# A two-layer selective scan over eight images: the short scan's gate in place, its running sums from PSUM, its result stored once per half, and the next image's map loaded inside the scan

## The chip, the cores and the metric

The kernel runs on one core of one Trainium2 chip. The metric is the device time of one launch in microseconds (us). Three runs of the kernel before took 12600.73, 12612.84 and 12614.98 us; their median is 12612.84 us. One further execution was recorded by the hardware profiler; it took 12615.41 us, and its span, from the first instruction to the last, is 12613.3 us.

The engines go by these names in the profile: PE is TensorE (matmul), PEld its weight loads, DVE is VectorE, ACT is ScalarE, POOL is GpSimd, and SP is SyncE, which here issues nearly all DMAs. Each engine works through its own instructions in order. SBUF is the on-chip memory, PSUM the memory that matmuls write.

## What is computed

Eight images of 64 x 64 positions and 96 channels pass two layers. Each layer normalizes, projects to 2 x 192 channels, convolves (3 x 3, each channel alone), and scans the 4096 positions in four directions (rows, columns, and both backwards) with 16 states for each of the 192 channels. Then come a layer norm, a gate by `silu(z)`, a projection back to 96 channels, and the sum with the input. The two layers differ in the scan. The first is an exact recurrence; the second divides running sums by a decay, which is cut off by a small constant:

```python
# layer 0, per step
dA = jnp.exp(d_t[..., None] * A)
h = dA * h + d_t[..., None] * B_e * u_t[..., None]
y_t = jnp.sum(h * C_e, axis=-1)

# layer 1, one direction; s1 = rows, s3 = columns
def _ssm_scan(u, ...):
    dt = jax.nn.softplus(dt @ dt_proj_w + dt_proj_b)
    A = -jnp.exp(A_log)
    log_dA = jnp.einsum('bld,dn->bldn', dt, A)
    dB_u = jnp.einsum('bld,bln->bldn', dt, B_mat) * u[..., None]
    decay = jnp.exp(jnp.cumsum(log_dA, axis=1))
    h = decay * jnp.cumsum(dB_u / (decay + 1e-12), axis=1)
    y = jnp.einsum('bldn,bln->bld', h, C_mat)
    return y + u * D_skip
...
y = y1 + y2 + back(y3) + back(y4)
y = _layernorm(y, ln_g, ln_b).reshape(B, H, W, D_INNER)
return (y * jax.nn.silu(z)) @ out_proj_w
```

In layer 1 the term `decay / (decay + 1e-12)` dies away along the sequence, so the kernel scans only the first 160 positions of each direction (fewer for the faster states), and multiplies them by a gate, `0.5 * (1 + tanh(0.5 * (A * cumsum(dt) + log 1e12)))`. This is the **short scan**. At the end the kernel looks at the smallest decay that it met and, should the cut not have been allowed, computes the second layer again in a general way; with these inputs that part doesn't run.

## The kernel before

**Tiling.** The 192 channels are two halves `h` of 96, and each half three groups `g` of 32. A group's 32 channels times 4 states fill 128 partitions, and a **set** is one group with 4 of the 16 states over 1024 positions. One image's long scan (layer 0) has 4 directions x 4 stretches x 2 halves x 3 groups x 4 sets = 384 sets. From the second image on (`b >= 1`), 6 **short sets** follow (2 halves x 3 groups), which are the layer-1 scan of the image before; a short set holds all 16 states in 960 positions. Images are numbered 0 to 7 here.

**The order.** `scan_rows` (from L408) writes the order of the work out by hand. Step `n` issues, for each engine, the stages of neighbouring sets: loads for set n+5 (`fetch`, L509), the decay of set n+1 (`fill`, L843: ScalarE, into one of two PSUM tiles), `drive` of set n+1 (ScalarE copies the input term into a single PSUM tile), `release` of set n-4 (ScalarE copies the finished sums out of the accumulator `acc`, of which there is one), `gate` of set n+1, the multiply and scan of set n (`advance_set`: VectorE, L892, L895, L898, L903), the product with C of set n-1 (`read_out`: GpSimd, L920, into one of four tiles `out`), and the sum over states of set n-3 (`collect`: TensorE, L933 and L956, into `acc`). Then come the stages that `plan` holds for that step: they prepare later work on the same engines.

**Jobs.** A half of a stretch is a job of 12 sets. While the sets of job m run, the job m+2 is prepared, by `ready` for long and `short_ready` (L719) for short jobs. The steps of `short_ready` count from the job's start; the two short jobs are prepared from steps 359 and 371. Its matmuls all use one PSUM bank (`pmisc`, tag `mm`). At steps 6 and 7 TensorE forms dt in that bank (`total`, L760), at steps 7 and 8 ScalarE copies it to `ln` (`delta`, L769), at step 9 GpSimd multiplies it by the input (`product`, L772) and VectorE forms both running sums from `ln` (`running`, L781, 320 elements each, one of them backwards), at step 10 ScalarE copies the sums' heads and scales their ends (`lowest`, L505 and L794), and at step 11 they are stored to DRAM. From there `fetch` loads them back, replicated over the states, as `dt_rep`, `dtu_rep` and `cum_rep`; the first two have two buffers each.

**The gate.** `gate` (L858) takes one of the four `out` tiles, writes the gate into it (L869), and L895 multiplies the set by it. `read_out` then uses the same tile for its product.

**The short result.** `release` copies `acc` to a tile `y_short` (L974, one buffer) and stores its four quarters to `ys_far` in DRAM by four DMAs of SP (L978). In the phase between the images `short_sum` loads `ys_far` back in one DMA (L1750), and `patch` (L1712, from step 7 of that phase) adds it.

**The convolution beside.** `conv_beside` computes the convolutions of layer 0 for the next image and of layer 1 for the image before, in pieces, during the scan, in the same `pmisc` bank: nine taps in three steps (L1023), ScalarE's curve (L1033), VectorE's product out of the bank (L1036), and a store to `xc_far` in DRAM. `windows` says at which steps; the two last pieces of images 1 to 6 start 9 steps into the jobs that begin at steps 359 and 371.

**Between the images.** `between` loads the next image's map from `xc_far` in four quarters (L1767), at steps 0, 9, 11 and 13, and runs `out_phase`: 16 chunks of 512 positions (8 of layer 0 of this image, 8 of layer 1 of the one before) through stages with fixed lags: sum (GpSimd, L1580), mean (TensorE, L1516), centring (VectorE, L1593), square, variance and so on. Beside them `first_deltas` prepares the next scan; its first stages are the projection of the next map (L560) at steps 2 and 3. After the last image `finish` takes the place of `between`; it has no next map.

## Time and profile before

| what | value |
|---|---|
| median of three runs | 12612.84 us |
| profiled execution | 12615.41 us |
| VectorE's running sums of the short jobs (L781) | 28, 789 to 7414 ns |
| short gates (L869) | 168 instructions, 423 to 923 ns |
| ScalarE idle before L869 until an `out` tile | 45.4 us in 14 waits |
| ScalarE idle before L974 until a store of `y_short` | 70.4 us in 21 waits |
| TensorE idle before L560 until the map | 64.7 us in 6 waits |
| TensorE's granted clock, mean | 0.80 |

A group row of the profile reads: line, engine, operation, output `<-` inputs with their shapes, count, then the busy time and the mean of one in ns, then the idle time before and what ended it. A row in order of time reads: start, duration, engine, line, operation, output `<-` inputs, count of merged instructions, and in brackets the idle time before with what ended it. "SPq" is the queue of SyncE, whose rows are issues of DMAs. In the table by stretch a row has the stretch, its length, the busy time of each engine, then TensorE's granted clock, the mean busy share of the 16 DMA engines and their GB/s. The releaser is inferred, and may be wrong where an instruction waits for several things.

One image takes about 1540 us, of which the scan with its short sets is about 1390 and the phase between about 150.

### The profile page before, as it was taken

To read this page: it belongs to the slowest core of one execution; us is meant where nothing else is said; L and a number is where in the kernel's file an instruction comes from. 1 tells how busy PE (TensorE), PEld (TensorE's weight loads), DVE (VectorE), ACT (ScalarE), POOL (GpSimd) and SP (SyncE) were. 2 spreads that over 40 slices of the span, in tenths; PEclk is the share of its full clock that TensorE was granted. 3 is DMA by queue.
4 is the path that set the end of the run, shared out by engine and by line. 5 is a ranking of instruction groups with operands and counts; after the bars stand their busy time and mean duration, and the time that the engine had idled before them with its cause. 6 is when DMAs were issued, how large, how long until landed. Compare 5 with 4: busy or idle time off the path is not lost. (4 is left out here: it accounts for less than half of the span.)

```text
span 12613.3 us, 134470 instructions
## 1 busy us (share of the span) xinstructions
PE 9519.2 (75%) x44284; PEld 3021.0 (24%) x44284; DVE 11031.8 (87%) x6870; ACT 9693.0 (77%) x15131; POOL 10513.1 (83%) x4802
## 2 busy tenths in 40 slices
PE   5875588876887778887788777887688886786566
PEld 1221122222222222222222222222222222222122
DVE  6999899996999969999699987999779997899966
ACT  4888778786888868878688877888778886788864
POOL 3999899995999859998699977999779996799964
PEclk8877788787888778877888878888788787887676
DMA  3444444444444444444444444444444444444430
GB/s 95 164 158 154 137 150 160 157 158 131 164 158 162 141 131 163 162 157 149 138 165 153 159 147 136 164 158 160 148 141 164 148 153 143 144 162 157 155 112 23
DMA packets 667346, 1853.80 MB, mean 147 GB/s; under 512 B 186840, under 2 KB 199262, under 8 KB 666541
## 3 DMA queue, kind: packets, MB, share of 16 engines
q1 hardware_dynamic: 659469, 1832.53, 44.1%
q10 hardware_dynamic: 7168, 12.59, 0.3%
q8 instruction: 351, 5.75, 0.2%
q14 instruction: 358, 2.93, 0.1%
HBM read 1533.82 MB, written 311.02 MB: 146 GB/s over the span
## 5 line engine op out<-in xcount | busy, mean ns | idle before, releaser
L920 POOL TENSOR_TENSOR out<-set,c_rep 128x1024 f32<-128x1024 f32 x3114 | 7290.0, 2360 | 954.3 <-PE acc L956 305.2
L903 DVE TENSOR_TENSOR_SCAN set<-decay,state,set 128x1024 f32<-128x1024 f32 x2304 | 5365.5, 2345 | 416.3 <-ACT decay L856 198.8
L856 ACT ACTIVATE decay<-dt_rep,w_a 128x1024 f32<-128x1024 f32 x3072 | 3419.3, 1114 | 298.5 <-DVE set L903 292.6
L892 DVE TENSOR_TENSOR set<-drive,b_rep 128x1024 f32<-128x1024 f32 x2346 | 2812.5, 1199 | 44.1 <-DMA b_rep<-x_dblr 33.6
L1023 PE MATMUL ps_conv<-edged,taps 96*96 96x512 f32 (+1 forms) x4032 | 2418.1, 739 | 30.3 <-ACT z L615 27.8
L956 PE MATMUL acc<-out,w_gather 128*32 128x256 f32 x24576 | 2285.0, 482 | 21.4 <-POOL out L920 21.3
L903 DVE TENSOR_TENSOR_SCAN set<-decay,set 128x1024 f32<-128x1024 f32 x768 | 1744.9, 2286 | 222.1 <-ACT decay L856 143.7
L882 POOL TENSOR_TENSOR set<-dtu_rep,b_rep 128x1024 f32<-128x1024 f32 x768 | 1809.5, 2356 | 99.0 <-DMA b_rep<-x_dblr 47.5
L947 PE MATMUL acc<-map,w_eye 96*32 96x256 f32 x4608 | 570.3, 577 | 1591.9 <-ACT map L986 1359.1
L986 ACT COPY map<-acc 32x256 f32<-32x256 f32 x3072 | 1470.9, 479 | 46.6 <-PE acc L956 6.0
L956 PEld LDWEIGHTS acc<-out,w_gather 128*32 128x32 f32 x24576 | 784.6, 131 | 1954.4 <-issue 1256.1
L1023 PEld LDWEIGHTS ps_conv<-edged,taps 96*96 96x96 f32 (+1 forms) x4032 | 713.3, 196 | 1345.3 <-issue 1211.7
L914 ACT COPY state<-set 128x1 f32<-128x1 f32 x2304 | 426.3, 185 | 758.2 <-DVE set L903 751.3
L634 PE MATMUL ps_sp<-z,w_eye 96*96 96x512 f32 x960 | 644.0, 758 | 305.6 <-ACT ln L643 256.0
L655 POOL TENSOR_TENSOR dtu<-ln,map 96x1024 f32<-96x1024 f32 x256 | 670.6, 2620 | 236.5 <-DVE ln L651 133.1
L875 ACT COPY drive<-dtu_rep 128x1024 f32<-128x1024 f32 (+1 forms) x810 | 808.0, 998 | 35.0 <-DMA dtu_rep<-dtu_far 32.1
L602 PE MATMUL ps_dt<-x_dbl,w_dtw 7*96 7x512 f32 x1024 | 589.9, 657 | 311.9 <-ACT z L615 151.0
L947 PEld LDWEIGHTS acc<-map,w_eye 96*32 96x32 f32 x4608 | 102.1, 122 | 2059.0 <-ACT map L986 1757.0
L634 PE MATMUL ps_sp<-dtu,w_eye 96*96 96x512 f32 x960 | 552.5, 660 | 0.0
L634 PE MATMUL ps_sp<-ln,w_eye 96*96 96x512 f32 x960 | 537.8, 644 | 0.0
L614 ACT ACTIVATE dt<-ps_dt 96x512 f32<-96x512 f32 x512 | 303.0, 592 | 276.8 <-PE ps_dt L602 257.3
L634 PE MATMUL ps_sp<-dt,w_eye 96*96 96x512 f32 x960 | 508.9, 613 | 0.0
(236 smaller groups left out, 9622.7 us busy)
## 6 DMA issues: line engine op xcount, KB each, us to landing
dt_rep<-dt_far SPq DMA_DIRECT2D x768, 512.0 KB
dtu_rep<-dtu_far SPq DMA_DIRECT2D x768, 512.0 KB
b_rep<-x_dblr SPq DMA_DIRECT2D x256, 512.0 KB
c_rep<-x_dblr SPq DMA_DIRECT2D x256, 512.0 KB
b_rep<-x_dblc SPq DMA_DIRECT2D x256, 512.0 KB
c_rep<-x_dblc SPq DMA_DIRECT2D x256, 512.0 KB
dt_far<-ln SPq DMA_DIRECT2D x256, 384.0 KB
dtu_far<-dtu SPq DMA_DIRECT2D x256, 384.0 KB
```

Source lines behind the costliest of these rows:

```text
L634: nc.tensor.matmul(job["ps"][:C, :], w["eye"], job[term][:, halves[s]], start=i == 0, stop=i == 3,)
L655: nc.gpsimd.tensor_tensor(like(job["dtu"], col), like(job["dt"], col), positions(xc[:, h, :], col, t0, T), ALU.mult,)
L856: nc.scalar.activation(s["decay"], s["group"]["dt"], AF.Exp, scale=rate)
L875: nc.scalar.copy(s["group"]["drive"], s["group"]["dtu"])
L882: nc.gpsimd.tensor_tensor(s["buf"], s["group"]["dtu"], b, ALU.mult)
L892: nc.vector.tensor_tensor(s["buf"], s["group"]["drive"], b, ALU.mult)
L903: nc.vector.tensor_tensor_scan(ordered(s["buf"], unit), ordered(s["decay"], unit), ordered(s["buf"], unit), 0.0 if unit["nth"] == 0 else s ...
L920: nc.gpsimd.tensor_tensor(s["out"], s["buf"], s["unit"]["c", s["i"]], ALU.mult)
L947: nc.tensor.matmul(acc, lhs[:, GC * g : GC * (g + 1)], positions(old[:, h, :], unit["column"], unit["t0"] + at, n), start=True, stop=False ...
L956: nc.tensor.matmul(acc, w["gather"], s["out"][:, at : at + n], start=False, stop=s["i"] == NS - 1, skip_group_check=True,)
L986: nc.scalar.copy(yk, like(acc, unit["column"]))
L1023: nc.tensor.matmul(job["ps"][:C, :], taps[l][:k, h, tap, :], edged[:k, tap // 3 : tap // 3 + rows, tap % 3 : tap % 3 + WW], start=tap == 0 ...
```

## The change

Five things change, all at the end of an image's scan or at the start of the phase that follows.

1. `gate` writes in place over the replicated running sums (`cum_rep`); L895 reads them from there. `read_out` takes an `out` tile for short sets as it does for long ones.
2. `running` reads dt from the PSUM bank and not from `ln`. The backward half is summed at step 8, straight from the bank that `total(1)` left; for the forward half a new matmul with the identity (`again`, step 8) brings `ln` into the bank again, and its sum follows at step 9. As the bank is in use longer, the last two convolution pieces of images 1 to 6 start one step later (`at + 10`).
3. `release` gathers the three groups of a half in one tile, which shares its buffer with `conv_out`, and stores it by one DMA when the third is there. `ys_far` changes its layout, and `short_sum` loads it by six DMAs, at steps 2 and 3.
4. The next map's four quarters are loaded by SP at steps 376, 378, 380 and 388 of the scan (`next_map`), and no more in `between`.
5. The four stages of the first projection in `between` come one step earlier.

```diff
@@ scan_rows
-                    release(at(-4), y, work)
-                    gate(at(1), work)
+                    release(at(-4), y, beside)
+                    gate(at(1))
@@ short_ready
+        def again(s):
+            job["v"] = bank(s, "ps_again")
+            lhs, src = w["eye"], job["ln"][:, halves[s]]
+            nc.tensor.matmul(job["v"], lhs, src, start=True, stop=True)
+
         def running(s):
-            if s == 0:
+            if s == 1:
                 job["cum"] = tile_of("dt0")
-            at = slice(0, 2 * HEAD)
+            src, out = job["v"][:, : 2 * HEAD], job["cum"][:, halves[s]][:, : 2 * HEAD]
             if s == 1:
-                at = slice(BLOCK + 2 * HEAD - 1, BLOCK - 1, -1)
-            nc.vector.tensor_tensor_scan(
-                job["cum"][:, at], ones_reset, job["ln"][:, at], 0.0, ALU.mult, ALU.add
-            )
+                src, out = src[:, ::-1], out[:, ::-1]
+            nc.vector.tensor_tensor_scan(out, ones_reset, src, 0.0, ALU.mult, ALU.add)
...
             (8, lambda: delta(1)),
+            (8, lambda: running(1)),
+            (8, lambda: again(0)),
             (9, product),
             (9, lambda: running(0)),
-            (9, lambda: running(1)),
@@ gate, advance_set, read_out
-            s["out"] = work.tile([P, T], F32, name="out", bufs=4)[:, :HT]
...
-                nc.scalar.activation(out, src, AF.Tanh, bias=half_log, scale=rate)
+                nc.scalar.activation(cum, cum, AF.Tanh, bias=half_log, scale=rate)
...
-            nc.vector.scalar_tensor_tensor(buf, s["out"], 1.0, buf, ALU.add, ALU.mult)
+            nc.vector.scalar_tensor_tensor(
+                buf, s["group"]["cum"], 1.0, buf, ALU.add, ALU.mult
+            )
...
-            if not s["unit"]["short"]:
-                s["out"] = work.tile([P, T], F32, name="out", bufs=4)
+            s["out"] = work.tile([P, T], F32, name="out", bufs=4)[:, : s["unit"]["n"]]
@@ release
-            part = work.tile([P, HEAD], F32, name="y_short", bufs=1)
+            if g == 0:
+                unit["y"] = beside.tile([P, MM], F32, tag="conv_out", name="y_short")
+            part = unit["y"][:, g * HEAD : (g + 1) * HEAD]
             nc.scalar.mul(part, s["group"]["acc"][:, :HEAD], 0.5)
-            dst = ys_far[unit["b"]][GC * g : GC * (g + 1), h, :]
-            for k in range(K):
-                at = slice(k * HEAD, (k + 1) * HEAD)
-                nc.sync.dma_start(dst[:, at], part[GC * k : GC * (k + 1), :])
+            if g == NG - 1:
+                nc.sync.dma_start(ys_far[unit["b"]][h], unit["y"][:, : NG * HEAD])
@@ windows
-                found.append((at + 9, (3, 3, 3), 1))
+                found.append((at + 10, (3, 3, 3), 1))
@@ beside
+    def next_map(b, i):
+        if i == 0:
+            maps[b] = keep.tile([C, NH, L], F32, name="map")
+        at = slice(i * T, (i + 1) * T)
+        nc.sync.dma_start(maps[b][:, :, at], xc_far[b][:, :, at])
...
+                for i, step in enumerate((376, 378, 380, 388)):
+                    plan.setdefault(step, []).append(lambda i=i: next_map(b + 1, i))
@@ short_sum
-        put(1, nc.sync.dma_start, ys, ys_far[b])
+        def load_sums(h, g):
+            dst = ys[GC * g : GC * (g + 1), h, :].rearrange("c (k a) -> c k a", a=HEAD)
+            src = ys_far[b][h, :, g * HEAD : (g + 1) * HEAD]
+            src = src.rearrange("(k c) a -> c k a", c=GC)
+            nc.sync.dma_start(dst, src)
+
+        for h in range(NH):
+            for g in range(NG):
+                put(2 + h, load_sums, h, g)
@@ between
-        xc = keep.tile([C, NH, L], F32, name="map")
+        xc = maps[b + 1]
...
-            put(0, load, 0)
...
-            for i in range(1, NT):
-                put(7 + 2 * i, load, i)
...
-                steps = (2, 3, 3, 4) + (4, 5, 5, 6, 6, 7, 7, 6, 8, 9, 9)
+                steps = (1, 2, 2, 3) + (4, 5, 5, 6, 6, 7, 7, 6, 8, 9, 9)
```

## The prediction

> **What bounds the kernel now.** I read the page's first part, then the groups of instructions, then the order of time on each engine at one place where the changed code runs (the end of the second image's scan, 2820 to 2980 us), then the same place in the other images, and last the busy time by stretch for the DMA share. The page's chain of waits puts 0% on everything and says nothing.
>
> ```profile
> span 12613.3 us, 134470 instructions
> PE 9519.2 (75%) x44284; PEld 3021.0 (24%) x44284; DVE 11031.8 (87%) x6870; ACT 9693.0 (77%) x15131; POOL 10513.1 (83%) x4802
> L781 DVE TENSOR_TENSOR_SCAN dt<-ones_reset,ln 96x320 f32<-96x320 f32 x28 | 106.3, 3835 | 0.8 <-PE ps_sp L760 0.8
> ```
>
> VectorE is the bound: in the long scan it goes without a pause from multiply (1.20 us) to scan (2.35 us). The changed code runs only in the last 31 of an image's 390 sets and at the entry of the phase between two images. So the average is of no use; VectorE (DVE) there:
>
> ```profile
> 2875.98 1.20 DVE L892 TENSOR_TENSOR set<-drive,b_rep 128x1024 f32<-128x1024 f32 x1
> 2877.28 2.35 DVE L903 TENSOR_TENSOR_SCAN set<-decay,state,set 128x1024 f32<-128x1024 f32 x1
> 2879.54 7.30 DVE L781 TENSOR_TENSOR_SCAN dt<-ones_reset,ln 96x320 f32<-96x320 f32 x2
> ...
> 2926.82 1.16 DVE L895 SCALAR_TENSOR_TENSOR set<-out,set 128x960 f32<-128x960 f32 x1 [3.99 <-ACT out L869]
> 2928.01 2.20 DVE L898 TENSOR_TENSOR_SCAN set<-decay,set 128x480 f32<-128x480 f32 x2
> ...
> 2935.15 1.16 DVE L895 SCALAR_TENSOR_TENSOR set<-out,set 128x960 f32<-128x960 f32 x1 [3.89 <-ACT out L869]
> ```
>
> Two running sums hold VectorE 7.30 us. The gates of short sets 5 and 6 are 4 us late. ScalarE (ACT) and TensorE (PE) say why:
>
> ```profile
> 2919.15 2.36 ACT L986 COPY map<-acc 32x256 f32<-32x256 f32 x4
> 2924.77 2.02 ACT L869 ACTIVATE out<-cum_rep,half_log,a_half 128x640 f32<-128x640 f32 x4 [3.26 <-POOL out L920]
> 2933.10 2.02 ACT L869 ACTIVATE out<-cum_rep,half_log,a_half 128x640 f32<-128x640 f32 x4 [3.26 <-POOL out L920]
> 2941.78 0.30 ACT L974 ACTIVATE y_short<-acc 128x160 f32<-128x160 f32 x1 [2.91 <-DMA ys_far<-y_short]
> 2946.31 0.30 ACT L974 ACTIVATE y_short<-acc 128x160 f32<-128x160 f32 x1 [4.23 <-DMA ys_far<-y_short]
> ```
>
> ```profile
> 2921.61 3.07 PE L933 MATMUL acc<-out,w_gather 128*32 128x160 f32 x32 [15.58 <-ACT map L986]
> 2946.76 1.73 PE L933 MATMUL acc<-out,w_gather 128*32 128x160 f32 x32 [2.80 <-ACT y_short L974]
> 2948.42 1.96 PE L1516 MATMUL ps_mean<-y_sum,w_avg 96*96 96x512 f32 x4
> 2960.88 3.67 PE L560 MATMUL ps_proj<-map,w_wx 96*78 96x512 f32 x4 [10.51 <-DMA map<-xc_far]
> 2964.35 1.72 PE L1516 MATMUL ps_mean<-y_sum,w_avg 96*96 96x512 f32 x2
> ```
>
> Gate 5 starts 0.09 us after the 3.07 us collect of set 1 has ended (2921.61 + 3.07 = 2924.68): it waits for that collect to free one of the four `out` tiles, not for GpSimd (POOL), which the row names. Gate 6 waits likewise for set 2. After the gates a chain of collect, `y_short` copy and its store runs to 2948.5; TensorE, in order, then meets the projection, which waits 10.5 us for the map. SyncE (SP) issues that load late, behind 24 small stores:
>
> ```profile
> 2929.86 21.70 SPq L978 DMA_DIRECT2D ys_far<-y_short  x24
> 2954.34 0.59 SPq L1767 DMA_DIRECT2D map<-xc_far  x1
> ```
>
> The same pattern stands in images 2 to 7 (the last has no next map). In image 0, without a short scan, the map is in time.
>
> **What the skill says.** The Trainium skill, SBUF — State Buffer, Who interferes with whom: a VectorE instruction with two SBUF inputs contends with a GpSimd instruction that reads SBUF, one with a single SBUF input does not. The trace agrees: L781, both inputs in SBUF, takes 789 to 7414 ns, L892, one input in PSUM, an even 1.20 us. PSUM — Partial Sum Buffer, PSUM bank collisions raise a hardware error: accesses to a bank are to be ordered by semaphore; in the changed program as built the sum read from PSUM waits for ScalarE, so for the copy (L769) of the same bank; nothing before shows this wait. DMA: Bandwidth & Descriptors, Anatomy of one DMA (told of transfers issued from GpSimd): about 2 us are fixed, mostly the receipt; here, issued from SyncE, a copy that needs a 4 x 20 KB store complete waits 2.9 us. TensorE: Matmul & The Clock Gate, Part 1: an idle array runs at half clock; the same 32 matmuls take 3.07 us after a pause and 1.73 us in a run.
>
> **The change, part by part** (times in the frame of image 1).
>
> Running sums. Each pair costs VectorE 7.2 to 8.1 us now (2879.54 to 2886.77; the other 13 alike). From PSUM a sum should take its shortest time now, 0.79 us, 1.6 us a pair; L892 and L898 (1.14 us for 480, PSUM decay) show that one PSUM operand keeps GpSimd out. But the first sum now comes one step earlier and waits for the second L769 copy, behind four L986 copies. VectorE reaches that spot at 2824.79 and 2875.98; L769 ends at 2827.47 and 2877.94: waits of 2.7 and 2.0 us (3.4 for one of image 2, 4.1 in image 5, 5.0 in image 7). Behind the wait on VectorE stands the next set's multiply, and behind that GpSimd and ScalarE. So a pair saves 7.3 - 1.6 - 2.7 = 3.0 us, a little more or less by image: 6.2 an image. Bounds for the wait: 0 and 5. The added matmul (L760 rows, 0.7 to 1.0 us) waits for VectorE, but TensorE has idle time of 5 to 10 us there. What is late next is nothing: the decays are there.
>
> Convolution one step later. Its bank is needed for the copy of `ln`, so it starts at step 10. Its third part now comes behind a collect that waits for L986, and its product (L1036) one set later. The next job's first matmul needs that bank; ScalarE stands before L740 (3.17 us now) and the next decay is queued behind it. Step by step: L1036 ends 2853.0 instead of 2849.5, matmul 2.0, two reads 1.2, decay 1.1: 2857.4, where the scan now starts at 2854.33. Loss 2.7 to 3.1, I take 2.7, since a decay wait of 0.36 lies in it; bounds 0 and 4. Images 1 to 6 only.
>
> Gate in place. No new tile is taken, so gates 5 and 6 need no collect. Gate 5 follows L986 at 2921.5 (before: 2924.8), then decay 6 and drive 2.9, copy 0.3, gate 6 ends 2928.7 (before 2935.1); its last product leaves GpSimd at 2934.4 (before 2940.9). Gate and multiply cost what they did: the tile stays in SBUF.
>
> One store a half. The copies of sets 2, 3, 5 and 6 no longer wait for a store; that of set 4 waits for one of 240 KB, and its collect hides that. Collect chain: set 2 2926.9 to 2930.0, then set by set 2.25 to 3.5 us (1.73 or 3.07 + 0.3 + gaps of 0.2), set 6 ends about 2940.8 instead of 2948.5: 7.7 us an image. 24 issues of SP become 2; six loads instead of one in the next phase are 3 us of SP, with no one waiting (used at step 7).
>
> Map beside the scan. Four loads of 768 KB; by program order the first three are issued near 2860, where
>
> ```profile
> core 0: us, PE busy (x) PEld busy (x) DVE busy (x) ACT busy (x) POOL busy (x), PEclk, DMA share, GB/s
> 2860.00:2870.00 10.00, 6.20 (x37) 2.31 (x38) 6.07 (x4) 9.70 (x11) 6.56 (x3) 0.66 0.33 100
> 2910.00:2915.00 5.00, 0.00 (x0) 0.00 (x0) 4.86 (x4) 4.90 (x11) 2.21 (x1) 0.50 1.01 375
> ```
>
> the DMA is a third busy, though full at 2895 to 2920. The fourth stands on SP behind the last loads of the short sets and delays nothing but the stores, which have 10 us. The old map's last reader was 15 steps earlier. The projection then needs no wait. From first mean to third mean it was 15.9 us (2948.42 to 2964.35); image 0, with the map there, took 6.2 (1478.93 to 1485.11). With both projections now between the means I take 7.4: 8.5 us an image, images 1 to 6. In image 7 the first mean waited 5.9 us for a sum whose memory lay under `y_short`; that tile now lies elsewhere: 5.9. Image 0: 0.
>
> Sum: images 1 to 6: 6.2 - 2.7 + 7.7 + 8.5 = 19.7, times 6 = 118.2. Image 7: pairs 2.25 + 3.05 = 5.3, tail 7.5, sum 5.9: 18.7. Together 136.9. The profiled execution took 12615.41 us (2.1 outside its span): 12478.5. The median is 2.6 below it: 12476.
>
> **Rivals.** DMA at the entry: shares of 0.78 to 1.03 from 2955 to 2985 speak for the next loads (y1 768 KB, statistics pieces) coming late once the map no longer does; against it, they shrink by the map's 768 KB and have over 15 us of slack. If the entry gives 2 us instead of 8.5: 12476 + 6 x 6.5 = 12515. No toll: the wait before the first sum and the later convolution are covered: 2.7 + 4.7 more in images 1 to 6, 7 in the last: 12476 - 44 - 7 = 12425. Slower: the map loads meet the short sets' loads. At the 230 GB/s of 2955 to 2985, 3.1 MB are 13.5 us; the loads are two tiles deep, so a late set also delays the issue of the one after next: 27 us an image against the gains of 19.7, 6 x 7.3 - 18.7 = 25 more: 12638. It decides once the short sets' tiles come over 20 us late. The shares of 0.13 to 0.43 up to 2890 speak against it. The gates not leaving the collect (another tile limit in their place) would leave 12476 + 7 x 6 = 12518.
>
> **How the numbers follow.** Forecast 0.58; DMA at the entry or another tile limit 0.22; no toll 0.12; slower 0.05; nothing left 0.03. The likeliest gives 12476, its own range 12450 to 12505. The range 12425 to 12545 takes in both neighbours. About 0.2% (25 us) is what can be told from no change: faster 0.92, same 0.03, slower 0.05.
>
> **What would show it.** L781's successor at about 0.8 us with 2 to 5 us of idle before the first of each pair, released by L769; longer idle before L740; no gate waiting for a collect; one y copy an image waiting for a store; no wait of the projection for the map; about 12 us less from the sixth short set to the first mean. Wrong if the sums stay over 2 us, if sets 1 to 4 take over 5.6 us each, or if the steps after the third mean wait for DMA.

## The result, and the profile after

The changed kernel took 12407.86 us (median of 4 runs, 12379.51 to 12419.07), the kernel before in the same session 12606.78 us; the ratio is 0.9843 (95% interval 0.9819 to 0.9867). In a later session of five runs (e9_after_again below) it took 12425.08 us beside 12604.98, ratio 0.9852 (0.9838 to 0.9866). It is 1.5% faster, some 180 to 200 us. The forecast was 12476 us with a range down to 12425: the direction was right, the gain was put at 137 us and so too small, and the time fell below the range (in the later session it stood at the range's lower edge).

The page of the changed kernel, first part. VectorE (DVE) was busy 71.4 us less than before; the running sums alone lost 83.8, while the multiply by the gate rose by 9:

```profile
span 12402.2 us, 134216 instructions
PE 9540.3 (77%) x44312; PEld 3022.4 (24%) x44312; DVE 10960.4 (88%) x6870; ACT 9688.3 (78%) x15131; POOL 10508.3 (85%) x4802
```

The groups of instructions of the changed kernel that answer to the rows named in the prediction:

```profile
L787 DVE TENSOR_TENSOR_SCAN dt<-ones_reset,ps_sp 96x320 f32<-96x320 f32 x14 | 11.4, 817 | 35.6 <-ACT ln L769 35.6
L787 DVE TENSOR_TENSOR_SCAN dt<-ones_reset,ps_again 96x320 f32<-96x320 f32 x14 | 11.1, 790 | 0.0
L872 ACT ACTIVATE cum_rep<-cum_rep,half_log,a_half 128x640 f32<-128x640 f32 (+3 forms) x168 | 84.7, 575 | 0.6 <-DMA cum_rep<-cum_short 0.2
L980 ACT ACTIVATE y_short<-acc 128x160 f32<-128x160 f32 x42 | 12.7, 303 | 64.6 <-PE acc L937 49.7 <-DMA ys_far<-y_short 14.8
L560 PE MATMUL ps_proj<-map,w_wx 96*78 96x512 f32 x512 | 400.5, 919 | 47.5 <-ACT z L615 36.5 <-ACT x_dbl L571 9.6
```

Of the waits that the change was aimed at, one part is left: 14.8 us of the 70.4 that the y copies waited for stores. The sums cost 22.5 us in place of 106.3, and their new wait is 35.6 us over 14 pairs, 2.5 a pair. The gates wait 0.6 us in all. The y copies wait for a store 7 times, once an image, and the first projection no longer waits for the map.

The same place as before, the end of image 1's scan, in order of time. VectorE at the first pair of sums and at the later convolution:

```profile
2824.52 4.59 DVE L908 TENSOR_TENSOR_SCAN set<-decay,state,set 128x1024 f32<-128x1024 f32 x2
2830.96 0.82 DVE L787 TENSOR_TENSOR_SCAN dt<-ones_reset,ps_sp 96x320 f32<-96x320 f32 x1 [1.85 <-ACT ln L769]
...
2835.19 0.79 DVE L787 TENSOR_TENSOR_SCAN dt<-ones_reset,ps_again 96x320 f32<-96x320 f32 x1
...
2855.06 0.68 DVE L1040 SCALAR_TENSOR_TENSOR conv_out<-conv_out,ps_conv 96x512 f32<-96x512 f32 x1 [2.07 <-ACT conv_out L1037]
2855.66 1.21 DVE L895 TENSOR_TENSOR set<-drive,b_rep 128x1024 f32<-128x1024 f32 x1
2859.12 2.35 DVE L908 TENSOR_TENSOR_SCAN set<-decay,state,set 128x1024 f32<-128x1024 f32 x1 [2.24 <-ACT decay L861]
```

ScalarE (ACT) at gates 5 and 6 and at the y copy of the fourth set, and TensorE (PE) from the first short collect to the third mean:

```profile
2923.26 2.02 ACT L872 ACTIVATE cum_rep<-cum_rep,half_log,a_half 128x640 f32<-128x640 f32 x4
2928.23 2.01 ACT L872 ACTIVATE cum_rep<-cum_rep,half_log,a_half 128x640 f32<-128x640 f32 x4
2936.48 0.30 ACT L980 ACTIVATE y_short<-acc 128x160 f32<-128x160 f32 x1 [2.10 <-DMA ys_far<-y_short]
```

```profile
2923.33 3.07 PE L937 MATMUL acc<-out,w_gather 128*32 128x160 f32 x32 [14.89 <-ACT map L990]
...
2940.81 1.10 PE L1529 MATMUL ps_mean<-y_sum,w_avg 96*96 96x512 f32 x2
2941.74 1.88 PE L560 MATMUL ps_proj<-map,w_wx 96*78 96x512 f32 x4
2943.46 1.02 PE L1529 MATMUL ps_mean<-y_sum,w_avg 96*96 96x512 f32 x2
2944.88 1.94 PE L560 MATMUL ps_proj<-map,w_wx 96*78 96x512 f32 x4 [0.40 <-ACT x_dbl L571]
2946.66 1.02 PE L1529 MATMUL ps_mean<-y_sum,w_avg 96*96 96x512 f32 x2
```

First mean to third mean is now 5.85 us, in every one of images 1 to 6; before it was 15.5 to 17.1 us (16.5 on average). The first projection takes 1.88 us in image 1. Before it took 3.67, after a wait of 10.5.

To see where the time went, I split each image at three marks that both kernels have, from the first scan on: ScalarE's first copy of dt for the short scan (L769, before any changed instruction of that image acts), the first short set's multiply by the gate, and the first mean of the next phase. The next image's first scan on VectorE ends the last piece (in image 7: the end of the last instruction). Sums in us, each kernel with two traces (the second ones are e5_before_again and e9_after_again):

| stretch | before | changed | difference of the means | predicted |
|---|---|---|---|---|
| scan up to the first copy of dt (image 0: up to the first mean) | 10031.6, 10025.1 | 10004.8, 10025.1 | -13 | 0 |
| copy of dt to first gate, images 1 to 7 | 555.4, 554.4 | 533.1, 538.0 | -19 | -26 |
| first gate to first mean, images 1 to 7 | 329.4, 328.9 | 263.7, 262.2 | -66 | -60 |
| first mean to next scan, images 1 to 6 | 962.4, 980.3 | 884.9, 885.2 | -86 | -51 |
| the same, image 0 | 90.7, 101.6 | 93.1, 90.4 | -4 | 0 |
| first mean to the end, image 7 | 436.1, 428.6 | 416.6, 427.4 | -10 | 0 |

The sums and the tail came out near what was expected. The big miss is the entry of the phase between the images: 14.4 us an image instead of 8.5. The first line, where nothing was changed, scatters between 9982 and 10047 us over the sixteen traces of this study; what stands in it and in the last two lines is not a gain that can be claimed. Of the 200 us between the two pairs of traces 172 lie in the three lines where something was changed.

### The profile page after: what moved, and what is told of

Same layout as the page of the kernel before. It is cut to its first block, busy times and chain, and to the rows that moved or that the text cites. A ratio compares the mean times of both kernels' runs of the same rounds, so it can differ in the third digit from the quotient of the medians.

```text
span 12402.2 us, 134216 instructions
## 1 busy us (share of the span) xinstructions
PE 9540.3 (77%) x44312; PEld 3022.4 (24%) x44312; DVE 10960.4 (88%) x6870; ACT 9688.3 (78%) x15131; POOL 10508.3 (85%) x4802
## 5 line engine op out<-in xcount | busy, mean ns | idle before, releaser
L895 DVE TENSOR_TENSOR set<-drive,b_rep 128x1024 f32<-128x1024 f32 x2346 | 2811.1, 1198 | 43.1 <-DMA b_rep<-x_dblr 28.2
L1027 PE MATMUL ps_conv<-edged,taps 96*96 96x512 f32 (+1 forms) x4032 | 2476.3, 754 | 54.5 <-DVE dt L787 25.9
```

What stands on the lines that cost most here:

```text
L895: nc.vector.tensor_tensor(s["buf"], s["group"]["drive"], b, ALU.mult)
L1027: nc.tensor.matmul(job["ps"][:C, :], taps[l][:k, h, tap, :], edged[:k, tap // 3 : tap // 3 + rows, tap % 3 : tap % 3 + WW], start=tap == 0 ...
```

## The experiments

Each is timed beside the kernel before in its own session; differences between two experiments are taken from the ratios or, where smaller than the scatter of about 20 us, from the stretches above.

**Undoing one part at a time.** The four parts were put back one by one.

e1_map_late (loads and projection stages back):

```diff
-                for i, step in enumerate((376, 378, 380, 388)):
-                    plan.setdefault(step, []).append(lambda i=i: next_map(b + 1, i))
@@ between
-        xc = maps[b + 1]
+        xc = keep.tile([C, NH, L], F32, name="map")
+            put(0, load, 0)
...
+                put(7 + 2 * i, load, i)
-                steps = (1, 2, 2, 3) + (4,
+                steps = (2, 3, 3, 4) + (4,
```

> The changed kernel with the map's four loads and the four projection stages put back into the phase between the images. The prediction's own step (8.5 us in each of images 1 to 6) lets the time rise by 51 us, from 12408 to 12459. My theory now, from the two traces: taking the map's wait away is worth more, because TensorE (PE) is the engine that the entry hangs on and ran its next matmuls at half clock after the idle time; the stretch from the first mean to the next scan's first set should go back from about 147 to 160 us in images 1 to 6, 12.9 us each: 77 us, 12485. Rival: the map's loads beside the scan cost something in the scan (DMA), which comes back here: then less than 51 us, under 12459, with a shorter stretch before the short sets' first gate.

Measured: 12499.67 us, ratio 0.9915 (0.9900 to 0.9931): 79 to 91 us are lost against the two ratios of the changed kernel. First mean to next scan is 162.5 us in images 1 to 6 (147.5 in the changed kernel), 15.0 us an image; before the first gate nothing became shorter, so the rival falls. TensorE at that place in image 4 of e1_map_late:

```profile
7522.64 1.96 PE L1527 MATMUL ps_mean<-y_sum,w_avg 96*96 96x512 f32 x4
7531.76 3.67 PE L560 MATMUL ps_proj<-map,w_wx 96*78 96x512 f32 x4 [7.16 <-DMA map<-xc_far]
7535.22 1.92 PE L1527 MATMUL ps_mean<-y_sum,w_avg 96*96 96x512 f32 x2
...
7567.71 1.92 PE L1532 MATMUL ps_r<-r,w_pick 128*96 128x512 f32 x2
```

The wait is only 7.16 us, yet an image loses 15 on average. What follows the wait runs at half speed: the two instructions of the mean take 1.92 us, where the changed kernel's took 1.02, and so do those of `ps_r`, a stage further on, 36 us after the projection's start. This is not quite the entry of the kernel before: there the map's load stood behind 24 small stores, so that the first projection waited 10.8 and 11.2 us on average (two traces) and not 7.3.

e2_sums_late (sums at step 9 from `ln`, convolution at `at + 9`):

```diff
-            (8, lambda: running(1)),
-            (8, lambda: again(0)),
             (9, product),
             (9, lambda: running(0)),
+            (9, lambda: running(1)),
...
-                found.append((at + 10, (3, 3, 3), 1))
+                found.append((at + 9, (3, 3, 3), 1))
```

> The changed kernel with both running sums back at step 9, from SBUF, and the last convolution pieces one step earlier. The prediction's own steps (6.2 less 2.7 us in images 1 to 6, 5.3 in image 7) give back 26 us: 12434. The traces say 22 us from ScalarE's first copy of dt to the first gate, summed over images 1 to 7: 12430. Rival: the 27 us by which the changed kernel's trace is shorter before any changed instruction of an image belong to this part too; then about 12457, and the stretch from a scan's start to the first copy of dt is about 4 us longer in each image than in the changed kernel.

Measured: 12430.02 us, 0.9865 (0.9846 to 0.9885), and 554.9 us from the first copy of dt to the first gate (533.1 and 538.0 in the changed kernel). The part is worth 17 to 22 us. The untouched stretch is 10016, between the changed kernel's 10005 and 10025, so the rival falls.

e3_four_stores (a tile of one buffer, four stores a group, one load):

```diff
-            if g == 0:
-                unit["y"] = beside.tile([P, MM], F32, tag="conv_out", name="y_short")
-            part = unit["y"][:, g * HEAD : (g + 1) * HEAD]
+            part = beside.tile([P, HEAD], F32, name="y_short", bufs=1)
...
-            if g == NG - 1:
-                nc.sync.dma_start(ys_far[unit["b"]][h], unit["y"][:, : NG * HEAD])
+            for k in range(K):
+                at = slice(k * HEAD, (k + 1) * HEAD)
+                nc.sync.dma_start(dst[:, at], part[GC * k : GC * (k + 1), :])
```

> The changed kernel with y_short as one buffer and four stores for each group again, and one load of the sums in the next phase; the gate stays in place. By the traces six y copies stood 20.0 us apart from first to last before and 12.9 after, so the tail from first gate to first mean loses about 7 us in each of images 1 to 7: 50 us. In image 7 the wait of the first sum for the tile's memory comes back (5.9 us). Theory: TensorE then also runs the first 30 us of the last phase at half clock, so that image 7's stretch from first mean to the end goes back from 417 to 428 us or more: 12475 to 12483 in all. Rival (the prediction's own step: only the wait is lost): at most 7 x 7 + 6 = 55 us, 12463, and that stretch stays at 417 us.

Measured: 12475.91 us, 0.9895 (0.9879 to 0.9911). The y copies wait for stores again, 92.4 us in all (14.8 in the changed kernel), in the groups of e3_four_stores:

```profile
L978 ACT ACTIVATE y_short<-acc 128x160 f32<-128x160 f32 x42 | 12.8, 304 | 112.2 <-DMA ys_far<-y_short 92.4 <-PE acc L937 13.6 <-PE ps_mean L1529 6.0
```

The stretch from first gate to first mean grows by 46.6 us in sum. In image 7 the first mean waits 6.47 us for its sum again. First mean to end is 427.8 us, as the theory said; but the second trace of the changed kernel has 427.4 without that wait, so this number says nothing about the clock after it.

e4_gate_apart (the gate into an `out` tile):

```diff
+            s["out"] = work.tile([P, T], F32, name="out", bufs=4)[:, :HT]
...
-                nc.scalar.activation(cum, cum, AF.Tanh, bias=half_log, scale=rate)
+                nc.scalar.activation(out, src, AF.Tanh, bias=half_log, scale=rate)
```

> The changed kernel with the gate written to a tile of its own again, out of the four that the products use. Theory: gates 5 and 6 wait again for the collects of sets 1 and 2; gate 5 about 3 us later, gate 6 about 6.7 us later after the first gate, of which some 1.9 us vanish in the slack of the last collect: 4.8 us in each of images 1 to 7, 34 us, 12442, and 42 to 43 us from first gate to first mean instead of 37.5. Rival (the stores own the tail): under 1 us an image, at most 12415.

Measured: 12446.91 us, 0.9874 (0.9855 to 0.9892), 44.4 us an image from first gate to first mean (37.7 in the changed kernel). The gates' wait is back, in the groups of e4_gate_apart:

```profile
L874 ACT ACTIVATE out<-cum_rep,half_log,a_half 128x640 f32<-128x640 f32 (+3 forms) x168 | 84.8, 575 | 46.6 <-POOL out L925 35.8 <-issue 10.0 <-DMA cum_rep<-cum_short 0.5
```

e10_tail_both undoes e3's and e4's part together:

> The changed kernel with four stores a group and the gate in a tile of its own, both as before. The prediction's own step gives the two together 59.6 us (7.7 in images 1 to 6, 13.4 in image 7): 12468. The traces say 66 us for the stretch from first gate to first mean, and some 10 more from the half clock after the wait in image 7: 12474 to 12484. Rival (they add up as they stand alone, 68 and 39 us): 12515, and 53 us from first gate to first mean where the kernel before had 46.

Measured: 12492.02 us, 0.9909 (0.9894 to 0.9924), 67 us above the changed kernel of the same session. In the stretch from first gate to first mean the single undos cost 46.6 and 47.2 us and both together 78.3. Each of the two takes away a wait that the other's wait would otherwise hide: they don't add up. 48.9 us an image stand in that stretch, where the rival said 53; the time fits the reading of the traces (66 to 76 us), the prediction's step (59.6) is near, and the rival's 107 is out. The kernel before has 47.1 us an image there, 13 us less in sum; which other part of the change makes that difference stays open.

**Is it the wait, or the clock after it?** e6_busy_wait and e11_busy_short give TensorE work while it waits for the late map.

```diff
+    def keep_busy(ps, n):
+        src = taps[0][:C, 0].rearrange("p a b -> p (a b)")[:, :MM]
+        for _ in range(n):
+            nc.tensor.matmul(ps[:C, :], w["eye"], src, start=True, stop=True)
@@ projection
             unit["ps"] = pmisc.tile([P, MM], F32, tag="mm", name="ps_proj0")
+            if s == 0:
+                keep_busy(unit["ps"], busy)
```

> e1_map_late (12500 us) with 14 further matmuls of 96x512 ahead of the first projection, from images 1 to 6 on: work for TensorE while it waits 7 to 11 us for the map; their result is overwritten. Theory: the idle time is what drops TensorE to half clock for the 10 to 40 us after it, about 5 us of the 15 us an image that the late map costs; the wait stays, but the first ps_r comes some 39 us after the first mean instead of 44, and the time falls by about 30 us to 12470. Rival (the slow clock has another cause, and only the wait counts): 12495 to 12505, first ps_r at 43 to 45 us.

Measured: 12491.9 us beside 12621.01 for the kernel before in that session, 0.9898 (0.9882 to 0.9915). The 14 matmuls took 12 us and outlasted the wait; all the same the next scan came 155.5 us after the first mean instead of 162.5, and the first `ps_r` 35.0 us after it instead of 44.0. By the ratios the kernel is about 21 us faster than e1_map_late, where 30 were expected; the intervals overlap, so the theory rests on the stretches and not on the time.

> e1_map_late with 7 further matmuls ahead of the first projection (about 0.98 us each), which fit into the wait for the map; the 14 of e6_busy_wait took 12 to 14 us and so outlasted it. Theory: the wait of 7 to 9 us stays, the half clock after it goes: the next scan's first set comes 152 to 154 us after the first mean (162.5 with the late map alone, 147.5 in the changed kernel), the time is 12440 to 12460. Rival (the clock does not follow the idle time): 160 to 163 us, 12500.

Measured: 12467.85 us, 0.9891 (0.9875 to 0.9906), above the 12440 to 12460 expected. First mean to next scan is 153.7 us, as expected. The wait is filled and not shortened, in image 4 of e11_busy_short:

```profile
7482.50 6.25 PE L150 MATMUL ps_proj<-taps,w_eye 96*96 96x512 f32 x14 [0.45 <-DVE map L1611]
7488.94 1.94 PE L567 MATMUL ps_proj<-map,w_wx 96*78 96x512 f32 x4 [0.19 <-DMA map<-xc_far]
```

The projection starts at the same distance from the first mean (8.85 us here, 9.12 in e1_map_late) and takes 1.94 us instead of 3.67. So, by one trace of each, of the 15.0 us that a late map costs, 162.5 - 153.7 = 8.8 are TensorE's slow clock after it and 153.7 - 147.5 = 6.2 the wait. Traces with the changed kernel's entry lie between 144.7 and 148.3 us, so the split is uncertain by about 2 us. The times of e1 and e11 differ by 32 us (the intervals of their ratios meet); 8.8 x 6 would be 53.

Busy time by stretch shows the clock. Image 4 from the first mean on, in steps of 15 us, first e1_map_late, then e6_busy_wait, then the changed kernel:

```profile
7523.00:7538.00 15.00, 7.84 (x12) 1.93 (x10) 3.18 (x3) 2.84 (x4) 5.78 (x5) 0.64 0.95 217
7538.00:7553.00 15.00, 14.66 (x21) 3.35 (x19) 3.40 (x4) 4.16 (x7) 5.58 (x5) 0.50 0.61 152
7553.00:7568.00 15.00, 15.00 (x18) 3.59 (x18) 5.04 (x7) 11.42 (x14) 3.81 (x3) 0.50 0.37 105
```

```profile
7514.00:7529.00 15.00, 14.55 (x34) 5.25 (x33) 2.35 (x2) 2.19 (x3) 5.00 (x4) 1.00 0.88 215
7529.00:7544.00 15.00, 14.11 (x34) 3.66 (x33) 6.08 (x6) 8.47 (x13) 8.85 (x7) 1.00 0.64 156
7544.00:7559.00 15.00, 11.90 (x24) 3.33 (x23) 9.33 (x13) 14.88 (x19) 5.70 (x4) 0.92 0.66 161
```

```profile
7466.00:7481.00 15.00, 14.27 (x36) 3.96 (x33) 6.09 (x5) 7.93 (x12) 10.91 (x9) 0.94 0.90 228
7481.00:7496.00 15.00, 11.47 (x14) 2.29 (x12) 5.80 (x7) 11.00 (x14) 4.24 (x4) 0.50 0.79 193
7496.00:7511.00 15.00, 14.13 (x27) 4.12 (x27) 13.14 (x14) 12.58 (x17) 10.18 (x6) 0.88 0.17 52
```

In e1_map_late TensorE is busy for all but 0.34 of the last 30 us and stays at 0.50; with the wait filled it keeps 0.92 to 1.00 (in image 3 it fell to 0.78 in the second stretch and 0.76 in the third). In the changed kernel a slow stretch remains, 15 to 30 us after the first mean.

e14_steps_late takes back only the earlier projection stages:

> The changed kernel with the four projection stages one step later again, the map still loaded inside the scan. If the earlier stages carry part of the entry's gain, the next scan's first set comes 150 us or more after the first mean instead of 147.5, 15 us or more in all, 12430 or more; if the late map alone made the loss: 146.5 to 148.5 us an image, within 6 us of the changed kernel on the same chip.

Measured: 12393.65 us, 0.9831 (0.9809 to 0.9853), 146.9 us an image. The stages bring nothing that can be seen; the entry's gain is the map's.

**What causes the slow stretch that is left?** e7_no_y1 leaves out the loads of the second layer's convolved map, and its skip term is computed from another map:

```diff
-            nc.sync.dma_start(y1[:, :, at], xc1_far[b][:, :, at])
...
-            nc.scalar.mul(at, at, w["dsum1"][:, h : h + 1])
+            nc.scalar.mul(y1[:, h, at], other[:, h, at], w["dsum1"][:, h : h + 1])
```

> The changed kernel without the four loads of 768 KB of the second layer's convolved map in the phase after each scan; its skip term is computed from another map in memory. The DMA engines are full from 5 to 25 us after the first mean there, and TensorE falls to half clock from 12 to 34 us after it. If the DMA load drives the slow clock, or if late data limit that stretch, the slow clock goes and the first ps_r comes 8 to 10 us sooner than the 31 us of the changed kernel: some 60 us in all, 12350. Rival (neither): first ps_r at 29 to 32 us, 12390 to 12415.

Measured: 12427.85 us beside 12621.01, ratio 0.9842 (0.9826 to 0.9859), the changed kernel's own. Image 4 of e7_no_y1, second stretch of 15 us:

```profile
7516.00:7531.00 15.00, 13.99 (x20) 3.45 (x20) 5.45 (x7) 11.02 (x13) 4.13 (x4) 0.67 0.16 53
```

The DMA share there falls from 0.79 to 0.16, and the clock is still 0.67 (0.50 and 0.65 in images 2 and 1). The first `ps_r` comes 27.8 to 29.1 us after the first mean, 2 to 3 us sooner, but the next scan does not (148.4 us). So the DMA load is not what brings the slow clock, and late data cost the entry nothing.

e8_busy_tail fills TensorE's idle time ahead of the first short collect:

```diff
+            def busy():
+                keep_busy(pmisc.tile([P, MM], F32, tag="mm", name="ps_busy"), 24)
+            if total > K * NT * NH * NG * NS:
+                plan.setdefault(386, []).append(busy)
```

> The changed kernel with 24 further matmuls in the 15 us in which TensorE waits before the first short set's collect (images 1 to 7). If idle time is what lowers the clock, the collects of sets 1 and 2 take 1.7 us instead of 3.1, worth up to 1.9 us an image before the last product limits, and if the slow stretch 12 us after the first mean goes back to the same idle time, another 8 to 10 us an image: 12330 to 12400. Rival (that slow stretch has another cause): first ps_r stays at 29 to 32 us and the time at 12395 to 12410.

Measured: 12474.17 us beside 12621.01, 0.9878 (0.9861 to 0.9894), slower than the changed kernel. A matmul of 96x512 is two instructions, and 24 of them took 23.7 us in image 1 (20.8 in image 7) and held up the first collect; first gate to first mean grew by 52 us in sum. After it the collects took 1.73 us each. But the slow stretch after the first mean stood where it was (first `ps_r` at 29.4 to 32.8 us in five of the six images, 22.0 in the sixth). So that stretch does not come from the idle time before the collects. TensorE in image 1 of e8_busy_tail, where the clock falls:

```profile
2948.20 1.10 PE L1540 MATMUL ps_mean<-y_sum,w_avg 96*96 96x512 f32 x2
...
2951.23 0.50 PE L1522 MATMUL ps_zb<-gn_shift,zw 96*96 96x1 f32 x4
2952.07 1.99 PE L1540 MATMUL ps_mean<-y_sum,w_avg 96*96 96x512 f32 x2 [0.34 <-ACT zb L1523]
```

What brings it stays open. The traces leave one candidate that no run varied. In images 1 to 6 of the changed kernel the clock falls 11.4 to 13.1 us after the first mean, and four matmuls of one column (`ps_zb`) start 10.8 us after it. In e11_busy_short they start at 17.0 to 17.5 us, and the clock falls at 18.6 to 19.8 in five of six images. In e6_busy_wait they start at 22.9, and it falls there in one image of six, so they alone don't bring it.

**The two halves of the running sums' part.** e13_conv_later is e2_sums_late with `at + 10` kept:

> e2_sums_late (12430 us, 555 us in sum from the first copy of dt to the first gate) with the last convolution pieces at the later step all the same, so the price of that shift alone. The prediction's own step: 2.7 us in each of images 1 to 6, 16 us: 12446, 571 us. From the traces (48 us saved on the sums, 22 seen in the stretch): 26 us, 4.3 an image, 12456, 581 us. Rival (the shift costs nothing when the sums stand at step 9): 12430, 555 us.

Measured: 12461.89 us, 0.9882 (0.9863 to 0.9902), 592.1 us in the stretch (554.9 in e2_sums_late): 37 us, about 6 in each of images 1 to 6. VectorE in image 1 of e13_conv_later:

```profile
2861.10 0.68 DVE L1035 SCALAR_TENSOR_TENSOR conv_out<-conv_out,ps_conv 96x512 f32<-96x512 f32 x1 [1.75 <-ACT conv_out L1032]
...
2865.16 2.35 DVE L903 TENSOR_TENSOR_SCAN set<-decay,state,set 128x1024 f32<-128x1024 f32 x1 [2.24 <-ACT decay L856]
2868.43 2.35 DVE L903 TENSOR_TENSOR_SCAN set<-decay,state,set 128x1024 f32<-128x1024 f32 x1 [0.92 <-ACT decay L856]
```

VectorE waits for the convolution's own copy (1.75) and then for two decays (2.24 and 0.92); in e2_sums_late the only one of these waits is 0.36. That is 4.6 of the 6 us; the changed kernel has the same three waits in image 1 (2.07, 2.24 and 0.92).

**Scatter, and a version meant to be faster.**

> The kernel before once more, for a second trace. In the first one the stretch from a scan's start to the first copy of dt (image 0: to the first mean), where nothing was changed, sums to 10032 us, in the changed kernel and the four experiments to between 10001 and 10016. If that is scatter of one execution, the second trace has 10000 to 10020 here; if the kernel before is slower there for a reason, 10030 again.

Measured: 12627.88 us in its one run, and 10025 us in the untouched stretch: neither of the two answers cleanly. e7_no_y1 had 10047 there and e14_steps_late 9982 with the same instructions, so the stretch scatters by more than the difference in question.

> The changed kernel once more, beside the three others of this set, for a second trace and a better median. All theories: 12395 to 12420; the stretches from first gate to first mean 37 to 38 us, first mean to the next scan's first set 147 to 148 us, and the untouched stretch of the scan anywhere between 10001 and 10047 us in sum, as so far. In image 7 the first ps_r stood 19 us after the first mean in the first trace and 25 to 27 in three experiments with the same instructions there: if the clock in that place is chance, it is 25 or more here too as often as not.

Measured: 12425.08 us, just above what was expected; first gate to first mean 262.2 us in sum, first mean to next scan 147.5 us, the untouched stretch 10025. In image 7 the first `ps_r` stood at 28.3 us: the fast clock of the first trace in that place comes and goes between executions of one program.

e12_gate_first:

```diff
+                keep_busy(pmisc.tile([P, MM], F32, tag="mm", name="ps_busy"), 8)
...
+                    if n == K * NT * NH * NG * NS - 1:
+                        gate(at(1))
                     release(at(-4), y, beside)
-                    gate(at(1))
+                    if n != K * NT * NH * NG * NS - 1:
+                        gate(at(1))
...
+            lhs, src = w["eye"], job["ln"][:, halves[s]][:, : 2 * HEAD]
+            nc.tensor.matmul(job["v"][:, : 2 * HEAD], lhs, src, start=True, stop=True)
...
-            (8, lambda: running(1)),
-            (8, lambda: again(0)),
+            (9, lambda: running(1)),
+            (9, lambda: again(0)),
```

> A version meant to be faster than both: the changed kernel with (a) the first short set's gate ahead of the four copies of release on ScalarE, where VectorE waits 3.3 us for that gate: 2.3 us less in images 1 to 7, 16; (b) the backward sum at step 9 as well, behind a set of VectorE, so that it no longer waits 1.9 us for ScalarE's copy, but the forward one waits about 1 us for its matmul, now of 320 columns: 13 in all; (c) 8 further matmuls in the 15 us before the first short set's collect, so that the first collects run at full clock: 1.6 us in images 1 to 7, 11. Together 40 us: 12368. Rival (VectorE meets the next wait in each place): 12395 to 12410.

Measured: 12392.48 us, 0.9830 (0.9811 to 0.9849), against 0.9852 (0.9838 to 0.9866) for the changed kernel beside it: the intervals overlap, so it is not shown to be faster. Against e9_after_again the stretch before the first gate became 30 us shorter, and the one after it 24 us longer. VectorE in image 4 of e12_gate_first, after the first short set:

```profile
7414.33 1.16 DVE L909 TENSOR_TENSOR set<-drive,b_rep 128x960 f32<-128x960 f32 x1 [2.22 <-ACT drive L892]
7416.54 1.16 DVE L912 SCALAR_TENSOR_TENSOR set<-cum_rep,set 128x960 f32<-128x960 f32 x1 [1.05 <-ACT cum_rep L886]
```

ScalarE in turn waits there for the load of the second set's `dtu_rep` (0.42 us) and has put its four copies of release after the gate. The time of the first gate is given back at the second: the rival was right for most of it.

## Why the prediction was wrong

**Running sums.** Right in kind, and 6 us short: 0.79 and 0.82 us a sum, the first of each pair behind L769 (from SBUF one sum of each pair had taken 6.6 to 7.4 us, the other 0.8). The wait measured 2.5 us on average (2.7 was taken for image 1, where it was 1.85 and 1.89). VectorE saved 106.3 - 22.5 - 35.6 = 48.2 us against 42.5 predicted, and undoing the sums with the later convolution in place (e13 against the changed kernel) costs 54 to 59 us in the stretch. ScalarE no longer stands 82 us before the heads' copies.

**Convolution one step later.** Right in kind, too small: 2.7 us predicted with a bound of 4; about 6 measured in e13, and 4.9 seen in the waits of image 1. The step followed L1036, the matmul, the reads and the decay; it left out that VectorE, moved next to ScalarE's L1037, waits for that copy as well. The longer idle time that was forecast before L740 did not come: in image 1 it fell from 3.17 to 1.85 us, and ScalarE waits 6.32 us at L1037 instead, for the convolution's matmuls. The errors of the two parts nearly cancel: 26 us predicted, 17 to 22 measured.

**Gate in place and one store a half.** Right, with one cost left out. Gate 6 starts 24.9 us after the first gate's multiply instead of 31.6, 6.7 us earlier (6.4 predicted). The tail gained 66 us against 60; the three later collects came 2.2 to 2.4 us apart, at the lower end of the 2.25 to 3.5 used. "About 12 us less from the sixth short set to the first mean" was badly put: from the first gate it is 9.4 us in image 1, from the sixth set's multiply 2.9. The multiply by the gate did not cost what it did: the 42 of them took 74.2 and 75.4 us in the two traces, 65.1 and 65.5 before. Why stays open; the tail's gain stands all the same.

**Map beside the scan: the step that failed.** Predicted: 15.9 us from first mean to third mean fall to 7.4, 8.5 us an image and nothing after. Measured: 14.4 us an image by the traces, 15.0 in e1. Two terms were wrong. Up to the third mean 10.7 us went and not 8.5: image 1 was the model, with 15.9, where the mean of images 1 to 6 is 16.5; and 5.85 were left and not 7.4, since the 7.4 was formed after image 0's entry and not from the duration of the four instructions at full clock (1.88). And the account stopped at the third mean, so that what follows was put at nothing; there another 3.7 us an image went (from third mean to next scan 143.9 and 146.8 us in the two traces of before, 141.6 and 141.7 in those of the changed kernel). TensorE's slow clock after a wait was priced for the collects (3.07 against 1.73) and not for the 30 to 40 us of nearly unbroken matmul work behind the projection. That this work pays for a wait is shown on e1, where filling the wait gives back 7 to 9 us an image, most of it behind the third mean. In the kernel before itself the clock came back at different times: in the second trace it stayed at 0.50 from 15 to 45 us after the first mean in images 4 to 6, and there the next scan came after 164.7 to 167.0 us; in images 1 to 3 it was 0.73 or 0.74, and the next scan came after 160.3 to 161.3, though the waits for the map differ by only 0.9 us on average.

The entry is the main part of what was missed: 35 of the 63 us by which the stretches' difference, 200, exceeds 137. Of the rest, 7 us more lie in the tail, 7 us less in the sums, and 13, 4 and 10 in the stretches that scatter without a change.

**Image 7.** The 5.9 us of the first sum's wait went (first gate to first mean fell by 13 us, 13.4 predicted). Of the further 19.5 us of the first trace ten lay in the first 30 us, where the clock was 1.00 and not 0.50. They are no gain of the change: the second trace has only 1 us against the kernel before's second.

**The rivals.** "DMA at the entry" is refuted by the 14.4 us that the entry gave and by e7, "another tile limit" by the gates' 0.6 us of waiting. The slower case did not occur: with the map loads in the scan the short sets' stretch from copy of dt to first gate is not longer (533 to 538 us against 543 in e1). (The 230 GB/s from which its price was worked out is the first of three stretches, 230, 195 and 228; with their mean the 13.5 us would be 14.2.) "No toll" named 12425, near the measured time, for a wrong reason: both tolls are there, 35.6 us of waiting and 5 to 6 us an image for the convolution; the entry made up for them.

## What to carry to other kernels

Price a removed wait of TensorE as the wait plus what its clock costs in the work after it: sum the matmuls that follow, and look at the granted clock there in a place of the same kernel without the wait. Where a phase is bound by TensorE, this can exceed the wait itself (8.8 against 6.2 us in e1 and e11). Follow a shifted step on every engine that it touches; the convolution's own copy was the wait that was overlooked. And two fixes of one chain are valued together, since each alone undone cost 47 us and both 78.

## What the runs showed of the hardware

The Trainium skill, TensorE: Matmul & The Clock Gate, Part 1, states that some 3.4 us of sustained activity bring the full clock back. The traces here agree that idle time lowers it (in the 15 us from the first mean on, 0.64 with the wait in e1_map_late and 1.00 with it filled in e6_busy_wait, image 4), and differ on the return: in e1_map_late TensorE was busy for 14.66 and 15.00 of two stretches of 15 us at 0.50 throughout. Nor is unbroken work enough to hold it: in e8_busy_tail TensorE had worked from 2901.86 us on with gaps under 3 us, and its matmuls still fell from 1.10 to 1.99 us a pair at 2952. Neither the DMA load (e7) nor the idle time before the collects (e8) explains that stretch; filling the wait directly after the first mean with 14 matmuls kept it away in five images of six, with 7 in one (0.62 to 0.66 in the second 15 us of the others). By the one image of e8 without it, where the next scan came after 142.9 us and not after 145.3 to 148.4, it costs an estimated 4 us an image, and a next gain may lie there.
